# A pair's message, distance factors and distances among the last filter products of a graph network layer

## Chip, cores and metric

The kernel runs on one core of a Trainium2 chip. The metric is the device time of one execution in microseconds; what is compared are medians of several executions.

A core has a matmul engine (TensorE, PE in the profile; its weight loads are the row PEld), VectorE (DVE), ScalarE (ACT), GpSimd (POOL) and SyncE (SP). Each works through its own list of instructions strictly in order. DMA transfers are issued from these lists too, here from SP, POOL and at the start ACT. So the order in which the program emits its work is, for each engine, the order in which it is done, and an instruction that waits holds up all that stand behind it on its engine.

## What is computed

For each of 64 graphs with 256 nodes and 256 features: a layer norm with ReLU, and on its result `x` a gated update from two sources, a convolution along the nodes and a message that each node takes from the others.

```python
h = _bn(_conv1d(xc, conv1_w, 0), ...); h = relu(h)
h = _bn(_conv1d(h, conv2_w, 8), ...)            # 17 taps, 256 -> 256 channels
x_conv = transpose(relu(h + xc))
s = x @ w_se.T + b_se                           # 3 numbers for each node
sq = sum(s * s, axis=-1)
dist = sq[:, :, None] + sq[:, None, :] - 2.0 * einsum('bnd,bmd->bnm', s, s)
A = exp(-dist) * mask
msg = relu(x @ w_msg.T + b_msg)
x_nmp = einsum('bnm,bmd->bnd', A, msg)
x_in = concatenate([x_conv, x_nmp])
gi, gh = x_in @ w_ih.T + b_ih, x @ w_hh.T + b_hh
r, z = sigmoid(gi_r + gh_r), sigmoid(gi_z + gh_z)
return (1.0 - z) * tanh(gi_n + r * gh_n) + z * x
```

All of it is float32.

## The kernel before

**Tiling.** Graphs are worked on in pairs (32 of them, `i`), and pairs in batches of four (eight batches, `b`). The second convolution is done by a short Fourier transform: VectorE takes the signal of a whole batch apart into 16 frequency bins, PE multiplies each bin by the filter's value at that bin, and VectorE puts the result together. A bin has three real products (`kind`), two bins make one product group `products(b, m)`, eight groups make a batch. The filter's values at the bins, `filt`, are the same for all batches. They lie in DRAM, and `load_kind` fetches the part for one bin and kind into one of nine `wb` buffers, three bins ahead.

**The opening.** `filt` has to be made first. `filters(m, g, eng)` (line 707) does one of 57 steps: two matmuls of the taps with a constant matrix into a PSUM bank of the kind `acc` (five of these), a copy by ScalarE into one of six `fo` buffers (line 716), and a DMA to DRAM (line 717), issued by POOL and SP in turn. The steps are taken from the list `steps` in three passes `m`, by `filter_steps(n)`. Between them stand the layer norms, transposes and first convolutions of the first four pairs. Then `forward()` hands the odd and the even half of the transform to VectorE, 26 more filter steps are emitted, SP is told to fetch the first nine `wb` parts, and the last 17 filter steps follow (line 988), four of the second pass and thirteen of the third. After them the buffers of the opening are given up.

**Who orders the work.** The order is written out by hand; nothing reorders it later. Only VectorE's transform steps are placed by a small planner, `Pace` (line 236). It keeps an estimate of how far PE and VectorE have come (`pace.pe`, `pace.dve`), raised by a fixed rule for each matmul and each VectorE instruction. Steps wait in a queue. When VectorE work that depends on PE is to be emitted, `pace.vector(n, ready)` first lets out as many steps of the queue as by the estimate fit before `ready`, plus 0.3:

```python
        while self.queue and self.dve + self.queue[0][0] / 960.0 <= ready + SLACK:
            self.run()
        self.dve = max(self.dve, ready) + (n / 960.0 + 0.1 if n else 0.0)
```

`pace.flush(mark)` lets out all up to a mark, for example up to the end of the odd half.

**The three functions that the change moves.** `message(i)` (line 792) has eight matmuls of 259 columns in four PSUM banks (three of the kind `aux`, of which there are three, and one `acc`), four additions of the bias on VectorE, ten small ScalarE operations that lay the three numbers and their squares into `Z`, and two ReLUs. `embed(i)` (line 815) transposes `Z` in three blocks on PE, and ScalarE copies the result to `ZT`. `affinity(i)` (line 822) multiplies parts of `ZT` in four small matmuls (three `aux` banks, one `acc`), takes the exponential on ScalarE (line 830) and multiplies by the mask `ADJ` on VectorE (line 836). At its end, for the first two pairs, it calls `load_adj(i + 1)`: two DMAs on POOL into the one mask buffer, which the multiplications just read.

In the main loop these three stand between the product groups: `message` before group 0, `embed` before group 1, `affinity` before group 2. The result is used by `transpose_a` and `aggregate`, after groups 2 and 3.

Of the kernel before, what the change touches and what calls it, by code (L numbers as in the profile page):

```python
# [301 lines left out]
def kernel(  # L302
# [105 lines left out]
    def load_adj(i, eng=nc.gpsimd):  # L408
        if i >= B // G:
            return  # L410
        if i < BY_DMA:
            ADJ[i] = work.tile([P, G * MC, N], FP, name="adj")
            load_rows(ADJ[i], adj, i, eng)
            return
        ADJH[i] = late.tile([P, 2 * MC, W], U16, name="adjh")
        for q in range(2 * MC):
            eng.dma_start(out=ADJH[i][:, q], in_=ADJD[i][:, q])
# [109 lines left out]
    def acc():  # L527
        return psum.tile([P, W], FP, name="acc", bufs=5)
# [194 lines left out]
    def load_kind(b, n, kind):  # L723
        b, n = b + n // BINS, n % BINS
        if b < NB and (n < BINS - 1 or kind < 2):
            WB[b, n, kind] = work.tile([P, DC, D], FP, name="wb", bufs=9)
            m = n // len(PASSES[0])
            nc.sync.dma_start(out=WB[b, n, kind], in_=filt[m][:, 3 * (n - PASSES[m][0]) + kind])
# [63 lines left out]
    def message(i):  # L792
        MSG[i] = work.tile([P, G, MC, D + SE], FP, name="msg")
        for g in range(G):
            for c in range(MC):
                p = acc() if g * MC + c == 3 else aux()
                for k in range(DC):
                    mm(p[:, :D + SE], chunk(HT[i][:, k], g, c), w_msg[:, k, :], D + SE,
                       start=(k == 0), stop=(k == DC - 1))
                pace.vector(D, pace.pe + PSUM)  # L800
                nc.vector.tensor_add(MSG[i][:, g, c, :], p[:, :D + SE], b_msg)  # L801
        s = MSG[i][:, :, :, D:]
        flat = s.rearrange("p g c s -> p (g c) s")
        nc.scalar.mul(Z[:, 0, :, :SE], flat, -2.0)
        nc.scalar.activation(Z[:, 0, :, SE:2 * SE], flat, AF.Square)
        for c in range(MC):
            z = Z[:, 1 + c].rearrange("p (g x) s -> p g x s", x=MC)
            for x in range(MC):
                nc.scalar.copy(z[:, :, x, :SE], s[:, :, c])
                nc.scalar.activation(z[:, :, x, 2 * SE:KD], s[:, :, c], AF.Square)  # L810
        for g in range(G):
            nc.scalar.activation(MSG[i][:, g, :, :D], MSG[i][:, g, :, :D], AF.Relu)


    def embed(i):
        p = aux()
        for j in range(1 + MC):
            transpose(p[:, j * P:(j + 1) * P], Z[:, j].rearrange("p q s -> p (q s)"))
        nc.scalar.copy(ZT, p[:, :(1 + MC) * P])


    def affinity(i):
        E[i] = work.tile([P, G, MC, N], FP, name="e")
        for g in range(G):
            for c in range(MC):
                q = g * MC + c
                p = acc() if q == 3 else aux()
                rows_q = slice(q * Q, q * Q + KD)
                nc.tensor.matmul(p[:, :N], ZT[rows_q, :P], ZT[rows_q, P:], start=True, stop=True)  # L829
                nc.scalar.activation(E[i][:, g, c], p[:, :N], AF.Exp, scale=-1.0)  # L830
        pace.tensor(N)
        for g in range(G):
            for c in range(MC):
                pace.vector(N, pace.pe + ACT)
                e = E[i][:, g, c].rearrange("p (c h b) -> p c h b", c=MC, b=NW)
                nc.vector.tensor_mul(e, e, ADJ[i][:, g * MC + c].rearrange("p (b h c) -> p c h b", c=MC, b=NW))
        AT[i] = E[i]
        if i + 1 < BY_DMA:
            load_adj(i + 1)
# [113 lines left out]
    def filter_steps(n):  # L953
        for k in range(n):
            filters(*steps.popleft(), nc.gpsimd if len(steps) % 2 else nc.sync)
# [29 lines left out]
    for n in range(3):  # L985
        for kind in range(3):
            load_kind(0, n, kind)
    filter_steps(len(steps))
    stage_ctx.close()
    late = ctx.enter_context(tc.tile_pool(name="late", bufs=1, reuse_waits="tile"))  # L990
# [3 lines left out]
    for b in range(NB):  # L994
        i = b * PB
        nxt = i + PB
        message(i)
        pace.flush(odd)
        products(b, 0)
        embed(i)  # L1000
        products(b, 1)
        pace.add(fft.branch_back(Yv, T, 0))
        affinity(i)
        if b > 0:
            load_adj(i + 1)
        products(b, 2)
        if b > 0:
            finish(i - 1)
        else:
            transpose_a(i)  # L1010
        products(b, 3)
        pace.flush(even)
        if b == 0:
            norm(nxt)
        else:
            run(norm_steps(nxt + 1)[0])
        pace.add(fft.branch_back(Yv, T, 2))
        pace.add(fft.odd_back(Yv, T))
        aggregate(i)
        if b > 0:  # L1020
            join_adj(i + 1)
        else:
            nc.gpsimd.dma_start(out=w_hh, in_=hh_wT.rearrange("(k p) o -> p k o", p=P))
            nc.gpsimd.dma_start(out=w_ih, in_=ih_wT.rearrange("(k p) o -> p k o", p=P))
        products(b, 4)
        message(i + 1)
        products(b, 5, lambda i=i: embed(i + 1))
        pace.add(mix(fft.q_back(Yu, T), fft.odd_factors(Yv)))
        if b == 0:
            pace.add(norm_steps(nxt + 1)[0], normed[1])  # L1030
        affinity(i + 1)
        if b > 0:
            load_adj(i + 2)
            join_h(nxt)
        products(b, 6)
        if b == 0:
            transpose_a(i + 1)
            transpose_h(nxt)
        products(b, 7)
        pace.add(mix(fft.p_back(Yu, T), fft.q_factors(Yu)), scaled)  # L1040

        def join(j):
            pace.add(fft.join(Yu, Yv, T, slice(2 * G * j, 2 * G * (j + 1))))
            pace.add([(W, lambda o=o: residual(i + j, o)) for o in range(DC)], joined[j])
        join(0)
        pace.add(norm_steps(nxt + 2)[0], normed[2])
        join(1)
        if b == 0:
            turn_adj(3)
            keep_adj(3)  # L1050
        aggregate(i + 1)
        if b > 0:
            join_adj(i + 2)
        message(i + 2)
        pace.flush(normed[1])
        turn_h(nxt + 1)

        def wait():
            pace.flush(scaled)
            affinity(i + 2)  # L1060
            conv1(nxt, aux)
            pace.add(split_steps(nxt), halved)
            join(2)
            pace.flush(joined[0])
        gates(i, 0, wait, lambda i=i: embed(i + 2))
        if b == 0:
            transpose_a(i + 2)
            load_y(0)
        load_adj(i + 3)
        sort_h(nxt + 1)  # L1070
        turn_adj(nxt)
        keep_adj(nxt)

        def early():
            join_h(nxt + 1)
            pace.flush(normed[2])
            turn_h(nxt + 2)
        gates(i, 1, None, early)
        pace.flush(halved)
        conv1(nxt + 1)  # L1080
        join(3)
        pace.add(split_steps(nxt + 1), halved)
        pace.add(norm_steps(nxt + 3)[0], normed[3])
        aggregate(i + 2)
        join_adj(i + 3)
        pace.flush(joined[1])
        sort_h(nxt + 2)
        turn_adj(nxt + 1)
        keep_adj(nxt + 1)
        gates(i + 1, 0, lambda nxt=nxt: join_h(nxt + 2))  # L1090
        pace.flush(normed[3])
        turn_h(nxt + 3)
        pace.flush(halved)
        conv1(nxt + 2)
        pace.add(split_steps(nxt + 2), halved)
        pace.add(norm_steps(nxt + 4)[0], normed[0])
        finish(i)
        sort_h(nxt + 3)
        turn_adj(nxt + 2)
        keep_adj(nxt + 2)  # L1100
        gates(i + 1, 1)
        join_h(nxt + 3)
        message(i + 3)
        conv1(nxt + 3)
        pace.add(split_steps(nxt + 3), halved)
        if b + 1 < NB:
            forward()
        pace.flush(normed[0])
        pace.flush(joined[2])

        def wait():
            affinity(i + 3)
            turn_h(nxt + 4)
        gates(i + 2, 0, wait, lambda i=i: embed(i + 3))
        sort_h(nxt + 4)
        turn_adj(nxt + 3)
        keep_adj(nxt + 3)
        aggregate(i + 3)
        finish(i + 1)
        load_adj(nxt)  # L1120
        gates(i + 2, 1)
        join_adj(nxt)
        pace.flush(joined[3])
        gates(i + 3, 0)
        finish(i + 2)
        gates(i + 3, 1)
# [45 lines left out]
```

## Time and profile before

| | us |
|---|---|
| median of 4 runs | 1831.82 |
| the runs | 1835.99, 1831.60, 1830.68, 1832.04 |
| the profiled execution | 1835.99, its span 1834.2 |
| busy in the span: PE | 1795.1 (98%) |
| VectorE | 1366.2 (74%) |
| ScalarE | 727.2 (40%) |
| GpSimd | 219.5 (12%) |

In the timeline of the profiled execution the opening looks like this. The first matmuls start at 16.4 us. The 43 filter steps from 59 us on run until 104.5 us on PE. From about 76 us ScalarE's copies come one, two or four at a time with waits between them; the last seven come in a row, from 101.88 us. The nine fetches of `wb` stand on SP from 84.85 to 91.1 us. `message(0)` is on PE from 104.50 us, the first product group from 108.11, `embed(0)` at 113.47, the second group from 113.80, `affinity(0)` at 119.25 and the third group from 119.89. The gates of the first pair begin at 169 us. One batch takes 215.6 us.

How to read the profile: in a timeline row stand the start, the length, the engine, the line, the operation, output and input, the count of instructions merged into the row, and in brackets for how long the engine had been idle and what it waited for. The chain that ended last is followed back from the last instruction, at each step to what released it, or to the one before it on its engine. Time on this chain is time that the execution would be shorter without, until another chain becomes the longest.

### The profile page before, as it was taken

Reading aid. Unit: us, or ns where it says so; the run is one execution under the profiler, and the core shown is the slowest. Engines: PE = TensorE matmul, PEld = TensorE weight load, DVE = VectorE, ACT = ScalarE, POOL = GpSimd, SP = SyncE. Lnnn points to the kernel's source line nnn. Section 1 sums busy time; section 2 is a strip of 40 time slices with the busy share of each in tenths; the row PEclk is TensorE's granted clock in tenths of the full one; section 3 lists DMA queues with packets and bytes.
Section 4 is the critical chain, followed back from the end, with each engine's and each line's share of the span. In section 5 each row is a group of like instructions: output and inputs, shape, how many; then the busy total and the mean of one; then the engine's idle time right before and its main releaser. Section 6 shows DMA issues by size and latency. Waiting matters only on the chain.

```text
span 1834.2 us, 21882 instructions
## 1 busy us (share of the span) xinstructions
PE 1795.1 (98%) x7494; PEld 1110.9 (61%) x7494; DVE 1366.2 (74%) x2596; ACT 727.2 (40%) x1444; POOL 219.5 (12%) x357
## 2 busy tenths in 40 slices
PE   5989999999999999999999999999999999999998
PEld 3677444964559554784448745595546944487453
DVE  4879669795778849797597967888587984979422
ACT  2535541365323642255422553236432463224321
POOL 2210101200111011111012000110111110111000
PEclk9999999999999999999999999999999999999999
DMA  7777543754438444565347644384544744163011
GB/s 193 231 244 243 119 95 95 227 159 109 101 94 262 110 108 96 140 200 126 81 94 212 166 100 110 84 259 121 120 101 115 227 104 97 42 186 114 8 39 34
DMA packets 250482, 245.96 MB, mean 134 GB/s; under 512 B 142936, under 2 KB 176500, under 8 KB 250371
## 3 DMA queue, kind: packets, MB, share of 16 engines
q1 hardware_dynamic: 216634, 183.83, 36.9%
q0 software_dynamic: 30784, 58.07, 13.5%
q10 hardware_dynamic: 2953, 2.66, 0.7%
q8 instruction: 59, 0.97, 0.2%
q14 instruction: 52, 0.43, 0.1%
HBM read 156.56 MB, written 44.30 MB: 110 GB/s over the span
## 4 chain that ended last, share of the span: by engine, by line
PE 91%; issue 3%; DVE 2%; DMA 2%; POOL 1%; ACT 1%; SPq 0%; POOLq 0%; ACTq 0%; DVEq 0%
PE acc L517 77%; PE aux L517 10%; PE aux L521 2%; PE aux L829 1%; DMA x<-in_x_dram 1%; POOL filt L717 1%; DMA adjh<-halves_d 1%; DVE Yv L59 0%; DMA filt<-fo 0%; ACT hT L671 0%; DVE T L65 0%; DVE Yv L62 0%; DVE st L559 0%; POOL rstd L565 0%; DVE msg L801 0%
## 5 line engine op out<-in xcount | busy, mean ns | idle before, releaser
L517 PE MATMUL acc<-xnm,w_ih 128*128 128x512 f32 x768 | 353.1, 592 | 0.0
L517 PE MATMUL acc<-hT,w_hh 128*128 128x512 f32 x768 | 350.5, 592 | 0.0
L517 PE MATMUL acc<-Yv,w_ih 128*128 128x512 f32 x768 | 342.7, 596 | 1.9 <-ACT Yv L789 1.9
L517 PEld LDWEIGHTS acc<-Yv,w_ih 128*128 128x128 f32 x768 | 145.7, 191 | 185.5 <-issue 182.9
L517 PEld LDWEIGHTS acc<-xnm,w_ih 128*128 128x128 f32 x768 | 144.7, 190 | 176.0 <-issue 174.4
L517 PEld LDWEIGHTS acc<-hT,w_hh 128*128 128x128 f32 x768 | 143.9, 190 | 164.6 <-issue 154.3
L891 DVE SCALAR_TENSOR_TENSOR gn<-tr,gn 128x512 f32<-128x512 f32 x64 | 44.1, 689 | 202.4 <-ACT tr L889 202.3
L889 ACT ACTIVATE tr<-acc,b_rz 128x512 f32<-128x512 f32 x64 | 44.0, 687 | 355.2 <-PE acc L517 355.2
L925 POOL DMA_DIRECT2D out_dram<-y x62 | 38.2, 620 | 789.5 <-DVE y L924 764.3
L517 PE MATMUL acc<-V,wb 128*128 128x128 f32 x1024 | 124.8, 275 | 0.0
L517 PE MATMUL acc<-U,wb 128*128 128x128 f32 x1024 | 124.2, 276 | 0.0
L517 PEld LDWEIGHTS acc<-U,wb 128*128 128x128 f32 x1024 | 120.4, 192 | 3.5 <-DVE T L59 2.0
L59 DVE SCALAR_TENSOR_TENSOR V<-T,V 128x256 f32<-128x256 f32 (+2 forms) x224 | 121.5, 607 | 0.3
L517 PEld LDWEIGHTS acc<-V,wb 128*128 128x128 f32 x1024 | 119.5, 192 | 0.0
L517 PE MATMUL acc<-hT,w_c 128*128 128x512 f32 x228 | 106.9, 610 | 2.7 <-ACT hT L633 1.4
L517 PE MATMUL aux<-e,msg 128*128 128x256 f32 x464 | 104.9, 379 | 0.0
L517 PEld LDWEIGHTS aux<-e,msg 128*128 128x128 f32 x464 | 87.1, 190 | 17.7 <-issue 6.9
L565 POOL TENSOR_TENSOR rstd<-rstd,neg_half 128x4 f32<-128x4 f32 x32 | 37.4, 1168 | 465.4 <-DVE shift L567 335.2
L896 ACT ACTIVATE nn<-gn,bn_columns 128x512 f32<-128x512 f32 x64 | 46.2, 722 | 116.3 <-DVE gn L894 116.3
L517 PE MATMUL aux<-w_msg,hT 128*128 128x259 f32 x384 | 89.6, 382 | 0.0
L426 ACT COPY adj<-adjh 128x1024 uint16<-128x1024 uint16 x58 | 74.1, 1345 | 23.9 <-DMA adjh<-halves_d 23.9
L517 PEld LDWEIGHTS aux<-w_msg,hT 128*128 128x128 f32 x384 | 72.1, 190 | 17.5 <-issue 7.6
(163 smaller groups left out, 2705.6 us busy)
## 6 DMA issues: line engine op xcount, KB each, us to landing
wb<-filt SPq DMA_DIRECT2D x376, 256.0 KB
y<-in_x_dram POOLq DMA_DIRECT2D x64, 256.0 KB, 5.3
out_dram<-y POOLq DMA_DIRECT2D x62, 256.0 KB, 5.7
x<-in_x_dram SPq DMA_DIRECT2D x60, 256.0 KB
halves_d<-halves SPq DMA_DIRECT2D x116, 128.0 KB
adjh<-halves_d POOLq DMA_DIRECT2D x116, 128.0 KB, 5.2
hh<-halves SPq DMA_DIRECT2D x108, 128.0 KB
filt<-fo POOLq DMA_DIRECT2D x18, 252.0 KB, 5.2
```

Of the source, the lines that this page charges most:

```text
L59: return self.step(out, lambda: self.v.scalar_tensor_tensor(out, x, s, y, op0=ALU.mult, op1=ALU.add))
L426: nc.scalar.copy(v[:, j], u[:, j])
L517: nc.tensor.matmul(p, w, v, **kw)
L521: nc.tensor.transpose(p, v, ident)
L565: nc.gpsimd.tensor_tensor(t["rstd"], t["rstd"], neg_half, ALU.pow)
L717: eng.dma_start(out=filt[m][g * KG:g * KG + size].rearrange("k t c o -> (k t) (c o)"), in_=t[:size * kinds])
L829: nc.tensor.matmul(p[:, :N], ZT[rows_q, :P], ZT[rows_q, P:], start=True, stop=True)
L889: nc.scalar.activation(tr, pr, AF.Tanh, bias=b_rz[:, dc:dc + 1], scale=0.5)
L891: nc.vector.scalar_tensor_tensor(gn, tr, 1.0, gn, op0=ALU.add, op1=ALU.mult)
L896: nc.scalar.activation(nn, gn, AF.Tanh, bias=b_ih[:, 2 * DC + dc:2 * DC + dc + 1])
L925: eng.dma_start(out=rows(out, G * i + g), in_=row_tile(Y[i], g))
```

## The change

The first pair's `message`, `embed` and `affinity` are emitted among the last 17 filter steps: message, seven filter steps, embed, four filter steps, affinity, six filter steps. In the loop they are left out for batch 0, and are as before for the other batches. Their instructions and operands are the same. `load_adj(1)`, which `affinity(0)` issues, moves with it. So does the letting out of transform steps on VectorE: `message(0)` and `affinity(0)` call `pace.vector` where before the filter steps went through with no such call, and the odd half was flushed at once.

```diff
         for kind in range(3):
             load_kind(0, n, kind)
+
+    message(0)
+    filter_steps(7)
+    embed(0)
+    filter_steps(4)
+    affinity(0)
     filter_steps(len(steps))
     stage_ctx.close()
...
     for b in range(NB):
         i = b * PB
         nxt = i + PB
-        message(i)
+        if b > 0:
+            message(i)
         pace.flush(odd)
         products(b, 0)
-        embed(i)
+        if b > 0:
+            embed(i)
         products(b, 1)
         pace.add(fft.branch_back(Yv, T, 0))
-        affinity(i)
         if b > 0:
+            affinity(i)
             load_adj(i + 1)
         products(b, 2)
```

## The prediction

> **What bounds the kernel now.** I read the page first, then the chain that ended last, then its stretch around the moved code, then the waits and the timeline of that stretch. The page gives PE 98% of the span and 91% of the chain. From the second batch on the chain is PE and repeats every 215.63 us (339.55, 555.18, 770.81 for the same piece), and this change touches none of it. So all is decided in the first 230 us. The chain there, from 96.9 us (columns: start us, us, what):
>
> ```profile
> 96.90 4.88 DMA filt<-fo
> ...
> 101.88 0.59 ACT fo L716
> ...
> 102.51 2.06 PE acc L517 x8
> 104.57 2.83 PE aux L517 x12
> 107.40 6.23 PE acc L517 x52
> 113.63 0.33 PE aux L521 x3
> 113.96 5.36 PE acc L517 x48
> 119.32 0.42 PE aux L829 x3
> ...
> 119.96 5.55 PE acc L517 x48
> ```
>
> Up to 102.5 us the filter products' writes to DRAM set the pace: a filter product needs a PSUM bank, the bank needs ScalarE's copy into one of six `fo` buffers, the buffer needs its write landed. From 102.51 on PE runs without a gap until 210.7 us, so each matmul taken out between 104 and 120 us is worth its whole length. `aux ... x12` plus four matmuls hidden in the x52 piece are message(0); `aux L521 x3` is embed(0); the `L829` pieces are affinity(0).
>
> The waits from 58 to 115 us (the PE row from 76 to 108 us, the DVE row from 94 to 108; columns: total us, times, longest us) show who has room before 104 us:
>
> ```profile
> ACT fo L716 <- DMA filt<-fo: 18.4, 15, 2.2
> ...
> PE acc L517 <- ACT fo L716: 5.3, 5, 1.4
> ...
> DVE msg L801 <- PE aux L517: 8.8, 1, 8.8
> ```
>
> ScalarE waits 18.4 us for writes, PE 5.3 us for ScalarE, VectorE 8.8 us for the very message product that is moved. The timeline rows that carry the prices:
>
> ```profile
> 84.74 1.07 ACT L716 COPY fo<-acc 126x512 f32<-126x512 f32 x2 [0.59 <-DMA filt<-fo]
> 86.79 1.07 ACT L716 COPY fo<-acc 126x512 f32<-126x512 f32 x2 [0.98 <-DMA filt<-fo]
> 89.38 1.06 ACT L716 COPY fo<-acc 36x512 f32<-36x512 f32 x2 [1.51 <-DMA filt<-fo]
> 92.60 0.58 ACT L716 COPY fo<-acc 77x512 f32<-77x512 f32 x1 [2.16 <-DMA filt<-fo]
> ...
> 101.88 3.50 ACT L716 COPY fo<-acc 77x512 f32<-77x512 f32 x7 [1.67 <-DMA filt<-fo]
> ```
>
> There are 57 filter steps. Counted back from the last copies, #51 to #57 are the x7 group, #46 is at 92.60, #44 (the 36-row one) and #45 at 89.38, #40 and #41 at 84.74. The change puts message(0) after #40, embed(0) after #47, affinity(0) after #51.
>
> **What leaves the path.** On PE, from the chain: message 2.83, plus the x52 piece less a pure 48-matmul piece, 6.23 - 5.36 = 0.87; embed 0.33; affinity 119.96 - 119.32 = 0.64, plus 5.55 - 5.36 = 0.19 of restart behind it. Sum 2.83 + 0.87 + 0.33 + 0.64 + 0.19 = **4.86 us**.
>
> **Message after #40.** In the weight-load rows filter #44 starts at 84.92 us at 0.87 to 0.9 us a filter, so #40 ends near 82.1; message then takes 82.1 to 85.7. PE is five PSUM banks ahead of ScalarE, so this eats its lead, not time. VectorE's order comes from the Pace counters. At message(0) they stand at pe 51.7 (40 filters 34.5, sixteen convolution products 13.8, 32 transposes 3.4) and dve 31.0 (the last convolution's 27.6 + 0.9, four split steps 2.5). The first sum lets steps out up to 51.7 + 0.9 of its products + 0.2 + 0.3 = 53.1: the odd transform's long ones bring dve to 48.15, and 13 of the 16 short ones (0.37 each) follow; two more go before the second sum, one before the third. The same counting of the old order gives eleven even steps ahead of the first sum, and the timeline has these eleven from 85.62 us. The 16 short steps run from 77.93 at 0.34 us each, so the 13th ends near 82.4 and VectorE waits some 0.7 us for the first product. The last sum lands near 86.1. ScalarE, behind copy #40 (ended 85.3), waits 0.8 us for it and then does ten small z operations and two ReLUs: 108.77 to 110.92 in the timeline, 2.15 us. Copy #41 comes at 88.3 instead of 85.3, #42 to #44 follow at 0.5 us each, #45 ends at 90.8 instead of 90.4, and #46 waits until 92.6 for a write either way. That wait hides the 3 us; without it they would be paid at the end. What is left: #42's write, on POOL, starts 1.1 us later (88.8 for 87.67). SP's writes do not move: SP issues the nine weight loads first and its write of #41 goes out at 93.50 in any case. If #42's buffer, taken again by #48, is late by the same 1.1 us and passes it on through the 96.90 write to #51, the price is 1.1. Bounds 0 and 1.1; I take 0, since DMA moves 297 to 392 GB/s from 88 to 96 us, and a write deferred leaves that room to the others.
>
> **Embed after #47.** Three transposes on an idle PE; ScalarE's `zT` copy (0.48 us at 114.00) goes between copies #47 (ends 95.37) and #48 (96.03, waiting for a write), a hole of 0.66 us. Cost 0, at most 0.5 if the hole closes.
>
> **Affinity after #51.** PE has `zT` at 95.9 and is done by 96.6. The four exponentials (119.98 to 121.20, **1.22 us**) stand behind copy #51, which waits for a write until 101.88, and in front of #52 to #57, which in the old order ran without a wait. Here is no cover: these six copies come 1.22 us later. The fourth product also takes a bank of `acc`, so filter #56 waits for that exponential (103.7) where it started at 102.51 behind #51's copy. The last filter ends 1.2 us later, near 105.8. So 1.22 us is paid. Lower bound 0, if #51's write lands earlier and some later copy waits instead; upper bound all of ScalarE's moved work, 2.15 + 0.48 + 1.22 = 3.85.
>
> **The queues passed.** affinity(0) issues load_adj(1), two DMAs on POOL that wait for the four mask products (2.11 us at 120.63). VectorE does seven even steps after Sv, to about 97.7, waits for the exponentials and finishes the masks near 105. Behind on POOL stand the writes of #52, #54 and #56; they go out 106.3 to 107.4 instead of 103.23 to 105.17. Nobody takes their buffers again, and the points they carry are fetched near 135 us. Two things meet them: the adjacency load (0.5 MB) and the fetches of the fourth bin. I book 0. VectorE itself gains: its 8.8 us wait becomes some 5.2 + 0.7, so it stays ahead by about as much as PE and does not become the bound. Behind the masks stand the rest of the even transform, 11.9 us of steps, and the first two groups' sums, 2.6; they end near 120, and their first taker is the fifth product group near 131 (135.04 before).
>
> **The sum.** 4.86 - 1.22 = 3.64 us. The profiled execution took 1835.99 us (span 1834.2 and 1.8 around it) and would take 1832.35; it is the slowest of the four runs. What is cut is a count of matmuls that does not grow with the run, so I take the same difference off the median: 1831.82 - 3.64 = **1828.2 us**. That is a gain of 0.20%, just about the 0.2% that a measurement of this kernel can tell from no change.
>
> The rows show that PE can lose its clock: from 45 to 48 us, after an idle stretch of 3.0 us ahead of 41.80, the granted clock was 0.50 and eight matmuls took 5.97 us where the same eight took 3.70 at 54.21. From 88 to 104 us, with gaps up to 1.4 us, it was 1.00, and the new gaps (up to 1.6 us around #53) are of that kind, so the sum holds no term for it. The Trainium skill, in "TensorE: Matmul & The Clock Gate", What's actually happening, says that an idle window of about 3.4 us halves the clock; by it, too, the sum stays, but were a gap to reach that length its warm-up of 3.4 us at half rate would cost an estimated 1.7 us.
>
> [...]
>
> **Rivals.** *More is hidden (0.12):* a copy after #52 has a wait of its own, and the exponentials fall into it. Full 4.86: 1827.0. For it: 15 of the copies waited for writes. Against: #52 to #57 did not. *More is exposed (0.16):* ScalarE's delay does not heal at #46. Gain between 4.86 - 3.85 = 1.0 and 4.86 - 1.22 - 1.1 = 2.5: 1829.3 to 1830.8. Against: waits of 2.16 and 1.61 us at #46 and #47. *Given back later (0.08):* the load of the fourth pair's adjacency, 9.28 us from 214.69 and part of the chain, has its own clock; then 1831.8. Against: POOL issued it just after the aggregate on PE, whose matmuls released its buffer, so it moves along. *Slower (0.17):* the second to fourth product groups run into the DMAs. A bin takes 0.79 MB per 2.68 us, 293 GB/s; PE decides above that, DMA below. If the late writes and the adjacency hold it to 202 GB/s (the mean from 95 to 110 us), a bin takes 3.9 us, 1.2 more, for six bins 7.3: 1831.8 - 3.6 + 7.3 = 1835.5. For it: 300 GB/s were moved here already. Against: PE did not wait for a `wb` once, nine bins' parts are fetched ahead, and up to 400 GB/s were reached.
>
> **How the numbers follow.** Forecast 0.47, its own range 1827.0 (nothing paid) to 1829.3 (1.1 more). Half of it, with its centre on the bound, and a little more for what the runs scatter, falls under faster: 0.37; with the first rival 0.49. Same: 0.10 of the forecast, 0.16 and 0.08: 0.34. Slower 0.17. The range, with a scatter of about 1 us: 1825.9 to 1831.3.
>
> **What will show it.** In the new chain PE's pieces go from filters straight to 48-matmul pieces with the first starting near 105.8 (108.3 before) and the third group near 116.5 (119.96). ScalarE's copy #46 stays near 92.6 and #51 near 101.9, exponentials directly behind it. VectorE waits 5 us for ScalarE's exponentials where it waited 8.8 for PE. It is wrong if #51 moves by more than 1 us, if PE waits for `wb`, or if the 215.63 us period changes.

## The result

The changed kernel takes 1829.84 us (median of 41 executions) against 1832.54 us (61): 2.70 us less, a ratio of 0.9986 with a 95% interval from 0.9981 to 0.9990, so between 1.8 and 3.5 us. Forecast were 3.64 us less, just outside that interval. It is faster, and by less than the 0.2% that was taken as the bound. The two profiled executions are not a fair pair: 1829.32 us is near its median, 1835.99 us is 3.5 us above its own.

The chain that ended last, of the changed kernel (start us, us, what):

```profile
91.36 6.57 DMA filt<-fo
...
98.00 0.59 ACT fo L716
98.59 0.04 issue
98.64 21.79 PE acc L517 x168
120.42 0.87 PE aux L521 x8
121.30 5.36 PE acc L517 x48
```

The pieces of message, embed and affinity are gone from between the filters and the products. The x168 piece is 24 matmuls of the last six filters and three whole product groups. But the last wait of the chain now ends at copy #48 (98.00 us) with six filters still to do behind it; before it ended at copy #51 with two filters behind it. The chain does not pass through the exponentials.

ScalarE's copies in the timeline of the changed kernel (start us, us, engine, line, operation, output and input, count, idle before it and what ended that):

```profile
83.78 0.58 ACT L716 COPY fo<-acc 126x512 f32<-126x512 f32 x1 [0.55 <-DMA filt<-fo]
...
88.10 2.71 ACT L716 COPY fo<-acc 126x512 f32<-126x512 f32 x5
91.09 0.58 ACT L716 COPY fo<-acc 77x512 f32<-77x512 f32 x1 [0.28 <-PE acc L517]
95.98 0.58 ACT L716 COPY fo<-acc 77x512 f32<-77x512 f32 x1 [4.30 <-DMA filt<-fo]
96.46 0.48 ACT L819 COPY zT<-aux 128x384 f32<-128x384 f32 x1
98.00 2.03 ACT L716 COPY fo<-acc 77x512 f32<-77x512 f32 x4 [1.07 <-DMA filt<-fo]
99.91 0.94 ACT L830 ACTIVATE e<-aux 128x256 f32<-128x256 f32 x3
100.72 0.41 ACT L830 ACTIVATE e<-acc 128x256 f32<-128x256 f32 x1
100.98 2.07 ACT L716 COPY fo<-acc 77x512 f32<-77x512 f32 x4
103.64 1.16 ACT L716 COPY fo<-acc 77x512 f32<-77x512 f32 x2 [0.60 <-DMA filt<-fo]
```

Copy #40 is the row at 83.78. Then ScalarE serves message, and #41 to #46 come as one block. All six buffers are full at once, their writes go out close together behind the nine weight loads, and #47 waits 4.30 us for the first of them to land. Single copies with short waits have become two blocks. The waits of 58 to 115 us (total us, times, longest us):

```profile
ACT fo L716 <- DMA filt<-fo: 10.7, 10, 4.3
...
DVE e L836 <- ACT e L830: 3.4, 1, 3.4
```

ScalarE waits 10.7 us for writes instead of 18.4. VectorE's 8.8 us wait for the message has become 3.4 us for the exponentials and 1.4 us for the message.

### The profile page after: what moved, and what is told of

Read it like the earlier page. It is cut to its first block, busy times and chain, and to the rows that moved or that the text cites. A ratio compares the mean times of both kernels' runs of the same rounds, so it can differ in the third digit from the quotient of the medians.

```text
span 1827.5 us, 21881 instructions
## 1 busy us (share of the span) xinstructions
PE 1793.5 (98%) x7494; PEld 1111.5 (61%) x7494; DVE 1366.3 (75%) x2596; ACT 726.9 (40%) x1444; POOL 219.5 (12%) x357
## 4 chain that ended last, share of the span: by engine, by line
PE 96%; DVE 1%; DMA 1%; issue 1%; ACT 0%; POOL 0%; SPq 0%; ACTq 0%; POOLq 0%; DVEq 0%
PE acc L517 82%; PE aux L517 11%; PE aux L521 2%; PE aux L829 1%; DMA x<-in_x_dram 1%; DMA filt<-fo 0%; ACT fo L716 0%; DVE Yv L59 0%; DVE T L65 0%; DVE Yv L62 0%; POOL rstd L565 0%; DVE y L924 0%; DVE x L571 0%; DVE msg L801 0%; DVE T L59 0%
```

## The experiments

The order of the emitted work is shown as a diff against the changed kernel. Each ratio is to the kernel before, on the same chip.

**Parts of the change alone.** Four kernels: message alone; message and embed; all three, with affinity behind the last filter; message alone with its ScalarE part left behind the last copy. The expectations name three theories of where some 2.2 of the 4.86 us went: the exponentials ahead of the last copies (X), ScalarE's delay around the message as well (Y), or something behind 104 us (Z). What a run does not move stays in the loop for the first pair too, as before; the split run moves the message alone.

```diff
 message alone
     message(0)
-    filter_steps(7)
-    embed(0)
-    filter_steps(4)
-    affinity(0)
     filter_steps(len(steps))
 message and embed
     embed(0)
-    filter_steps(4)
-    affinity(0)
     filter_steps(len(steps))
 affinity last
     embed(0)
-    filter_steps(4)
-    affinity(0)
     filter_steps(len(steps))
+    affinity(0)
 message split
         s = MSG[i][:, :, :, D:]
...
+        if i > 0:
+            factors(i)
+    def factors(i):
...
         if b > 0:
             message(i)
+        else:
+            factors(i)
```

> The change took 2.70 us off the median where 4.86 us of PE work left the path, so some 2.2 us came back. Only message(0) is moved here; embed(0) and affinity(0) stand where they stood before. Theory X (the four exponentials in front of the last six copies cost the 2.2 us): -3.7 us against before, all of message's PE time. Theory Y (ScalarE's 3 us around the message do not quite heal before the last copies, about 1 us of them stays, the exponentials cost the other 1.2): -2.7 us. Theory Z (the products start early enough, and about 1 us is given back after 104 us, where the fetches of wb meet the late writes and the mask): between -2.7 and -3.7 us, with waits of PE behind the first product.

> message(0) and embed(0) moved, affinity(0) and its mask load where they stood before. X: -4.0 us against before (3.70 + 0.33). Y: -3.0 us. Z: no mask load and no late writes on POOL here, so nothing is given back: -4.0 us, and better than the whole change by the 1.3 us.

> As the change, but affinity(0) behind the last filter step: its matmuls are on the path again (0.83 us), its exponentials no longer stand in front of a copy. X: -4.0 us against before. Y: -3.0 us. Z: the mask load is still early, so about as the change, -2.7 to -3.0 us.

> As the run with message(0) alone, but only its matmuls and its sums on VectorE are moved; its twelve ScalarE operations stand behind the last copy of the filter products. X: the same as message alone, -3.7 us. Y: ScalarE is not held up among the copies, so -3.7 us where message alone has -2.7. Z: the same as message alone.

| | ratio to before | 95% interval |
|---|---|---|
| the change | 0.9986 | 0.9981 to 0.9990 |
| message alone | 0.9980 | 0.9971 to 0.9989 |
| message and embed | 0.9983 | 0.9974 to 0.9992 |
| affinity last | 0.9983 | 0.9974 to 0.9992 |
| message split | 0.9982 | 0.9974 to 0.9991 |

The times do not separate the theories: the intervals are some 1.6 us to either side, and the theories lie about 1 us apart. Two things can be said. Message alone stands at 3.7 us in the middle of its interval (2.0 to 5.3), as booked for it, and no run with more moved stands above it. And taking ScalarE's part of message out of the way does not make it faster, which speaks, weakly, against theory Y. The profiles said more than the times. In the runs with message alone and split the last five filters behind the block of copies took 4.65 us; in the other two the same five took 6.34 us, though nothing that is moved lies among them.

**The cover taken away.** If the moved work gains because it lies in waits (theory P of the expectations), the gain must go when the waits go. Ten buffers for the copies instead of six, in the kernel before and in the changed one:

```diff
+    EXTRA = [work.tile([P, DC, W], FP, name="hT", bufs=6) for _ in range(2)]
...
-        t = stage.tile([P, W], FP, name="fo", bufs=6)
+        k = done.popleft()
+        t = stage.tile([P, W], FP, name="fo", bufs=6) if k % 10 < 6 else EXTRA[(k % 10 - 6) // 2][:, k % 2]
```

> The kernel before with ten buffers for the filter products' copies in place of six (four are taken from buffers for normalised pairs that are not in use yet); nothing else. If the wait for buffers is what made room, ScalarE and PE now run ahead: PE waited 5.3 us for ScalarE's copies, so -3 to -5 us against before. If the transfers' total (full share of the DMA engines from 86 to 98 us) sets the end of the opening, less than -1.5 us.

> The change with the same ten buffers. Theory P (the moved work was hidden in PE's and ScalarE's holes between the copies): where the holes are gone, the 4.86 us of PE work only stand in another place, so the same as the run before it with ten buffers, within 1.5 us. Theory Q (the opening ends when its writes are through, whatever PE and ScalarE do): still about 2.7 us faster than that run.

The kernel before with ten buffers takes 1824.28 us, 0.9956 (0.9943 to 0.9970); the changed one with ten takes 1824.00 us, 0.9955 (0.9942 to 0.9967). The chain of the kernel before with ten buffers:

```profile
79.96 14.41 PE acc L517 x65
94.37 2.83 PE aux L517 x12
97.20 6.23 PE acc L517 x52
```

and of the changed one with ten:

```profile
81.50 7.20 PE acc L517 x32
88.70 0.33 PE aux L521 x3
89.03 3.45 PE acc L517 x16
92.48 0.42 PE aux L833 x3
...
93.13 21.71 PE acc L517 x168
```

In both PE runs from 80 us on without a hole. The moved pieces stand on the chain in either place, and the third product group ends at 115.3 and 114.8 us. So theory P holds where it matters most: the change gains by filling holes, and where there are none it gains 0.3 us, which cannot be told from nothing (five executions of each, which scatter by up to 4 us). Theory Q, that the writes alone set the end of the opening, falls. The holes themselves are worth three times the change, and these are the fastest versions that were run.

**More work for ScalarE at the two places.**

```diff
 the exponentials four times
-                nc.scalar.activation(E[i][:, g, c], p[:, :N], AF.Exp, scale=-1.0)
+                for _ in range(4 if i == 0 else 1):
+                    nc.scalar.activation(E[i][:, g, c], p[:, :N], AF.Exp, scale=-1.0)
 the ReLUs four times
-        for g in range(G):
-            nc.scalar.activation(MSG[i][:, g, :, :D], MSG[i][:, g, :, :D], AF.Relu)
+        for g in range(G * (4 if i == 0 else 1)):
+            nc.scalar.activation(MSG[i][:, g % G, :, :D], MSG[i][:, g % G, :, :D], AF.Relu)
```

> The change with the first pair's four exponentials done four times over, 3 x 1.22 = 3.66 us more on ScalarE between copies #51 and #52. P: no cover there, so 3.66 us slower than the change, +1.0 us against before. Q: what is left of the copies after it waits for writes anyway (0.60 us at #56 in the changed trace), so well under 3 us slower than the change: 0 us against before or still faster.

> The change with the first pair's two ReLUs of the message done four times over, 3 x 1.14 = 3.42 us more on ScalarE between copies #40 and #41. P: the delay heals in the 4.3 us that copy #47 waits for a write in the changed trace, so within 1 us of the change, -1.7 to -2.7 us against before. Theory R (a hold-up of ScalarE at the message leaves buffers empty and writes late, and that is what came back of the 4.86 us): the full 3.4 us slower than the change, +0.7 us against before.

Exponentials: 1834.93 us, 1.0013 (1.0004 to 1.0022), slower than before and some 0.27% or 4.9 us slower than the change. Their place has little cover. In the timeline of that run PE stands and waits for them, and runs slowly behind:

```profile
99.55 4.69 ACT L831 ACTIVATE e<-aux 128x256 f32<-128x256 f32 x12
104.14 1.63 ACT L831 ACTIVATE e<-acc 128x256 f32<-128x256 f32 x4
```

```profile
98.27 3.68 PE L517 MATMUL acc<-taps,points 119*77 119x256 f32 x16 [0.62 <-ACT fo L716]
...
105.82 2.73 PE L517 MATMUL acc<-taps,points 119*77 119x256 f32 x8 [3.87 <-ACT e L831]
108.48 2.07 PE L517 MATMUL acc<-Sv,wb 128*128 128x128 f32 x8
110.35 3.62 PE L517 MATMUL acc<-V,wb 128*128 128x128 f32 x16
113.76 1.12 PE L517 MATMUL acc<-Sv,wb 128*128 128x128 f32 x8
```

The sixteen exponentials take 6.22 us where the four took 1.22, so 5.0 us were added and not 3.66. PE has filters to do for 1.1 of them and waits for 3.87. So P's "no cover" is not quite right: 1.1 us is about what the four exponentials take. And the times hold a second cost: behind the wait the granted clock fell to 0.50, the last two filters took 2.73 us where the kernel before has 2.06, and the first bin of products 5.28 us (108.48 to 113.76) where the changed kernel has 2.78. That is 3.2 us, and the 4.9 us of the medians can't be split cleanly between the two.

ReLUs: 1829.46 us, 0.9983 (0.9974 to 0.9991), no slower than the change, with 3.1 us more on ScalarE (the eight take 4.26 us, the two took 1.14). The hold-up at the message heals, as P has it, and theory R, that it costs its full length, falls. Copy #47 of that run still waits 4.43 us for a write.

**The same kernels again.** To see what an execution scatters, the kernel before was profiled twice more and the changed one once more:

> The kernel before once more, for a second profile: its profiled execution was the slowest of four. If the opening is what varies, the gap-free stretch of PE starts earlier than 102.5 us here and the span is shorter by as much; if not, the span differs and the opening does not.

> The kernel before a third time, for a third profile, with the same question: start of PE's gap-free stretch and of the first product group (108.3 us in the first profile) against the span.

> The changed kernel once more, for a second profile: start of the first product near 104.3 us if the opening is steady; the span minus that start tells what varies behind it.

| us | end of the last filter on PE | start of the transposes behind group 2 | second minus first |
|---|---|---|---|
| before | 104.57 | 125.35 | 20.78 |
| before, second | 102.36 | 123.14 | 20.78 |
| before, third | 101.92 | 122.71 | 20.79 |
| changed | 104.15 | 120.26 | 16.11 |
| changed, second | 106.01 | 122.12 | 16.11 |

(The first column is start plus length of the last row of filter matmuls, the second the start of the row in which E is transposed.) The difference of the last column is 4.67 us, the same in every pair. What varies is the end of the last filter. Its mean is 102.95 us before and 105.08 us after, 2.13 us later. 4.67 - 2.13 = 2.54 us, close to the 2.70 of the medians; but the first column alone scatters by 2.65 us over the three profiles before, so that it comes so close is luck. The medians are the better source: 4.67 - 2.70 = 1.97 us came back, between 1.2 and 2.9 by the interval. From those transposes to the aggregate of the third pair all five take 83.45 or 83.46 us, so nothing is given back there.

In the second profile of the changed kernel the last filters run slowly. Their row in the first profile, then in the second, and below them a table of the second by stretches (stretch, length, then busy time and instructions of PE, PEld, DVE, ACT, POOL, then the granted clock, DMA share, GB/s):

```profile
98.64 5.51 PE L517 MATMUL acc<-taps,points 119*77 119x256 f32 x24 [0.93 <-ACT fo L716]
```

```profile
97.64 8.37 PE L517 MATMUL acc<-taps,points 119*77 119x256 f32 x24 [0.52 <-ACT fo L716]
```

```profile
94.00:96.00 2.00, 0.61 (x3) 0.15 (x1) 1.90 (x4) 0.78 (x2) 0.00 (x0) 1.00 0.92 352
96.00:98.00 2.00, 1.25 (x9) 0.65 (x10) 0.00 (x0) 1.17 (x4) 0.12 (x1) 0.66 0.62 231
98.00:100.00 2.00, 2.00 (x6) 1.15 (x5) 0.65 (x2) 2.00 (x8) 0.93 (x2) 0.50 0.52 143
100.00:102.00 2.00, 2.00 (x7) 1.12 (x6) 2.00 (x5) 1.18 (x3) 0.26 (x1) 0.50 0.58 177
102.00:104.00 2.00, 2.00 (x7) 1.28 (x6) 2.00 (x5) 0.58 (x1) 1.55 (x4) 0.63 0.44 114
```

PE was busy 1.86 of the 4 us from 94 to 98, and the granted clock fell to 0.50. The 24 matmuls took 8.37 us; in the first profile of the same kernel, where the clock stayed at 1.00, the same 24 took 5.51. Of the eight profiles of kernels with message moved and six buffers, five show a drop near there: 6.34 for 4.65 us in two of the runs with parts, 6.96 for 5.51 with the ReLUs, 8.37 for 5.51 here, and the one with the exponentials, after its wait of 3.87 us. Of the three profiles of the kernel before one shows it (94 to 99 us), among copies that waited for writes anyway: its last filter ends at 102.36 us, between the other two.

How busy PE is does not by itself tell which profile drops. The first profile of the kernel before, in which the clock stayed at 1.00 (here the busy time of PE alone, then clock, DMA share, GB/s):

```profile
92.00:94.00 2.00, 0.77 (x4) 1.00 1.02 386
94.00:96.00 2.00, 0.90 (x5) 1.00 1.04 398
```

PE was busy 1.67 of these 4 us, less than the 1.86 above. In each of the eleven profiles with six buffers and no filled hole there are 4 us between 86 and 108 us with PE busy for less than 2; six of them drop and five don't.

**The hole filled.** The last run keeps PE busy where it waits for `zT`; the transposes it adds are read by nobody.

```diff
     filter_steps(4)
+    warm = aux()
+    for _ in range(18):
+        nc.tensor.transpose(warm[:, :P], ident, ident)
     affinity(0)
```

> The change with 18 transposes of the identity matrix (0.11 us each, nobody reads them) on PE ahead of affinity(0), where PE waits for zT after about 94.6 us. Theory C: with message(0) moved PE runs full until 94.6, then stands in two holes for most of 4 us; in five of eight profiles of such kernels the granted clock then fell to half for one or two stretches of 3.4 us, just when the last six filters have to run one behind the other, at a cost of 1.7 to 2.9 us; this is what brings the 3.6 us down to 2.7. Then here the clock stays at 1.00 from 94 to 104 us, the last six filters take 5.5 us and the time is 3.5 to 4.2 us below before. Theory P alone (1.22 us and more for the exponentials, the clock only scatters): as the change, -2.7 us, and the low clock may show here as well.

Measured were 1828.67 us against 1834.19 us on that chip, 0.9972 (0.9960 to 0.9983). The same stretch of this run, in its timeline:

```profile
93.11 3.62 PE L517 MATMUL acc<-taps,points 119*77 119x256 f32 x16
96.56 2.13 PE L995 MATMUL aux<-ident 128*128 128x128 f32 x18
...
99.38 5.51 PE L517 MATMUL acc<-taps,points 119*77 119x256 f32 x24
```

The clock is 1.00 in every stretch from 86 to 108 us and PE waits for nothing, in one profile; three of the eight profiles without the filler kept their clock too, so this alone shows little. The gain over before is 5.5 us (3.1 to 7.3), where theory C, that the clock takes the missing microsecond, had 3.5 to 4.2; the two intervals just overlap (0.9983 against 0.9981), so the gain over the change is likely and not settled. The profile does not show it: its last filter ends at 104.89 us, later than in the first profile of the change.

## Why the prediction was right, and where its size was off

**What leaves the path** was booked at 4.86 us and measured at 4.67. The difference is 0.19 us. About half of it is a restart that now falls to the first product: its first eight matmuls take 1.16 us behind the filters, 1.05 behind the message.

**Message after #40** went as worked out. VectorE let 13 short steps out, then two, then one; the last sum landed at 86.02 us (forecast 86.1); copy #41 came at 88.10 (88.3). "The delay heals by #46" was right in effect, as the ReLUs show, and not in form: the delayed copies came as a block, and the wait moved to #47. "SP's writes do not move" was wrong by 2.1 us: the write of #41 went out at 91.36, earlier than forecast, and the last wait on the chain is for its landing.

**Embed** was not seen to cost anything; `zT` was copied right behind #47. **The queues passed** were not seen to cost anything: the mask load went out on POOL at 102.76 and the three writes behind it from 104.00 us, PE did not wait for a `wb` in the changed kernel (once, 0.32 us, in the run with affinity last), and VectorE did not become the bound. Nor did the exponentials among the copies bring a load of ScalarE's function table: each of the two traces has one `ACT_TABLE_LOAD`, near 18 us. So the slower rival fell, and so did the one in which the gain is given back later.

**Affinity after #51.** That the end of the filter steps moves out was right; the road by which it does was wrong, and its size is the term that was off. Booked was the last filter 1.22 us later, for the exponentials; measured is some 2 us (1.97 by the medians, 2.13 on the mean of three and two profiles). "Here is no cover" is the step that failed. The forecast had PE five banks of PSUM (the memory that PE writes its products to) ahead when the last waiting copy came, so that only the six copies and the exponentials counted. In the changed kernel the copies come in blocks, #52 has to wait for the bank of #48, and the last six filters stand one behind the other on the chain: 5.51 us on PE. The exponentials lie beside them. Made four times as long they are the bound at once, so the 1.22 us were near the path but not on it.

By the forecast's own sign this part is wrong: #51 was to move by no more than 1 us. It came at 99.44 and 98.44 us in the two profiles of the changed kernel, against 101.88, 99.66 and 99.23 before. A cost that was not paid stood where another was, so that the sum came within 1 us is in part luck.

**The clock.** "The sum holds no term for it" is the sentence that failed. The forecast took the new gaps (1.6 us at most) for harmless, because gaps of nearly that length had been so in one profile. Two gaps of 1.3 to 1.6 and 0.5 to 0.9 us with 0.7 us of work between them were enough in one of two profiles of the changed kernel, and a drop costs 1.5 to 2.9 us, because behind it PE is the bound. One such drop in every two executions, 1.4 us on average here, would be more than the 0.9 us that are missing: without it the last filter would end at 104.15 and 103.15 us, 0.7 us later than before on the mean. That the drop occurs and what it costs is shown; how often it occurs over all executions, and so that it makes the difference between 3.6 and 2.7 us, is an inference from a few profiles and from the filled hole, and stays open.

The Trainium skill, "TensorE: Matmul & The Clock Gate", What's actually happening, names an idle window of about 3.4 us, free-running, as what throttles. The traces agree with the half rate and with stretches of about 3.4 us (1.7 us lost in each), but not with idle: PE was busy for nearly half of the 4 us ahead of the drop. That the same stretch drops in one execution and not in the next would fit a free-running window; no run here shows where the window lies.

One figure in the description of the time before was miscounted: from 57.75 us on there are 45 filter steps (two, 26 and 17), not 43. No term of the sum uses it.

## What to carry over

Work moved into another engine's waiting time gains only while that waiting lasts: with four more buffers the wait was gone, and the gain of the move with it, while the buffers themselves brought 8 us. When a steady trickle of waits is made into blocks, ask what has to run in series behind the last block; that, not the moved work, became the term here. And where PE is less than about half busy over some 4 us and is the bound right afterwards, allow for a clock drop: here it came in about half of the profiles, so one profile at full clock does not rule it out.

## What was not expected of the hardware

A PE wait of 1.9 us can halve the clock behind it. In the last batch every profile has one such wait, and the twelve matmuls behind it take either 5.42 us (six of fourteen profiles) or 7.0 to 7.12, here in the first profile of the kernel before (granted clock 0.50 from 1696 to 1698 us)

```profile
1694.33 7.11 PE L517 MATMUL acc<-Yv,w_ih 128*128 128x512 f32 x12 [1.88 <-ACT Yv L789]
```

and here in the run with message alone:

```profile
1686.39 5.42 PE L517 MATMUL acc<-Yv,w_ih 128*128 128x512 f32 x12 [1.89 <-ACT Yv L789]
```

The same instructions after the same wait differ by 1.69 us. The span behind the aggregate of the third pair (the PE row at 208.81 us in the first profile before) falls near 1622.2 or 1623.8 us in twelve of the fourteen profiles, and which of the two it is goes with this drop every time. The first profile before, at 1625.4, and the kernel before with ten buffers, at 1624.0 without the drop, have something else on top: soon after the aggregate PE waits there 1.1 and 1.4 us for ScalarE, which the other twelve profiles don't. So a part of the scatter of a kernel that does the same work each time is this: whether a short wait trips the clock or not.
